# One rotary projection, exchanged rows and late division in the attention stage with heads of 64

## The chip, the core and the metric

The kernel runs on one core of one Trainium2 chip. The metric is the device time of one execution in microseconds, lower is better. A core has five engines that run side by side, each with its own queue of instructions, executed in order: TensorE (PE in the profile, its weight loads are PEld), VectorE (DVE), ScalarE (ACT), GpSimd (POOL) and SyncE (SP), which here issues nearly all DMAs. They wait for each other on semaphores. TensorE writes only to PSUM, which is divided here into tiles of 512 float32 columns ("banks") handed out in turn.

## The reference, cut to what matters

The program is four pairs of a feed-forward layer and an attention layer around 2048 tokens of 128 features. The change touches only the last attention layer, with 16 heads of 64, a latent of 64 for keys and values, rotary embedding and a causal mask:

```python
x = x + _L3_attn_ref(_layernorm(x), ...)

def _L3_attn_ref(x, wq, w_kv_down, w_k_up, w_v_up, wo):   # in outline
    lat = x @ w_kv_down.T                       # 2048 x 64
    q = rope(x @ wq.T)                          # 16 heads of 64
    k = rope(lat @ w_k_up.T)
    v = lat @ w_v_up.T
    p = softmax(causal(q @ k.T / 8))
    return (p @ v) @ wo.T

rope(t) = t * cos + rotate_half(t) * sin        # rotate_half exchanges the two halves of a head (32 rows), with a sign
```

## The kernel before, in words

The kernel is one list of stages (`STAGES`): feed-forward and attention by turns. Each stage is a generator that can begin ("lead") while the stage before still runs. The stage in question is `attn3`; `ffn3` runs before it (its first half-step) and after it.

`attn3` keeps features on the partitions and tokens along the free axis. Two heads make a pair of 2 x 64 = 128 rows, so there are `NP` = 8 pairs, and 2048 tokens are `NC` = 4 chunks of `CH` = 512. The 32 iterations `its` are (pair, chunk of queries).

*Making queries and keys.* `make(m)` yields the pieces of work that produce the rotated queries and keys of iteration m. Before the change there are four pieces (`half(what, i)`): each of q and k is projected twice, once with the weights and once with weights whose rows are exchanged by halves (`swapped` on the host). A projection of q takes three matmuls of 512 columns (`product`, lines 227 to 229: the operands are split into a high and a low part), one of k takes two (`latents`, lines 1753 and 1754). VectorE multiplies each projection, out of PSUM, with the cosine or the signed sine (line 1791), GpSimd adds the two products (`whole`, line 1801), and later ScalarE and GpSimd split the sum into high and low parts (`high`, lines 1806 and 1807), which go to DRAM and come back as rows of the score operands (`load`, line 1867). The pieces are emitted by `fill`, one per `SPACE` of a clock that counts matmul columns, up to `AHEAD` iterations in advance; deferred parts (`timed`) come `LATER` after. The pieces of the first three iterations are made in the lead, before the stage proper.

*The flash loops.* `flash` runs two streams on TensorE. Stream A computes the scores once (line 1069) to find the maxima of each query: VectorE reduces each pair of PSUM tiles (line 1087, `tc.high_priority()`), out of two double-width PSUM tiles (tag `s1`). Stream B computes the scores again, transposed (line 1171), ScalarE exponentiates (line 1179, tile `pt`, six buffers), and TensorE multiplies with the latent values (line 1136, `pv`). The sum of the exponentials is kept per partition in `sum`, one addition per exponential tile (`on_exp`, line 1993), half of them on GpSimd, half on VectorE, and the last ones of an iteration all on VectorE. Score tiles of stream B, projections (`rot`), totals (`sums`) and output products (`py`) share one ring of three PSUM banks (tag `s2`).

*Finishing an iteration.* `finish` copies `pv` to `ov`; `total` adds the sums over partitions by two matmuls with ones (line 2006). ScalarE copies the result, and its two distinct rows go to DRAM, come back spread over the partitions, VectorE takes 128 x 8 reciprocals (line 2026), which go to DRAM and come back broadcast; VectorE multiplies `ov` (line 2036), TensorE multiplies with the folded output weights `wo` (line 2042) and VectorE adds to the residual `xs` (line 2045). Only the last iteration takes the reciprocal in place (`direct`).

The order on every engine is set by the emission order, by priorities and by explicit ordering (`in_order`); buffers in rings decide what waits.

Of the kernel before, what the change touches and what calls it, by code (L numbers as in the profile page):

```python
# [64 lines left out]
def tile_macaron(ctx: ExitStack, tc: tile.TileContext, a: dict, out: bass.AP, stages=STAGES):  # L65
# [904 lines left out]
    def flash(io, pool, early, its, nh, causal, scale, s1, s2, pv_mm, put_max, begin, finish, poll=None,  # L970
# [60 lines left out]
        last_top = {}  # L1031
        alive = [True]
# [16 lines left out]
        def stream_a():  # L1049
            for n, (g, qc) in enumerate(its):  # L1050
# [4 lines left out]
                for pi in range(npair):  # L1055
                    for r in range(TC):
# [3 lines left out]
                        for kc in range(2 * pi, min(2 * pi + 2, nk)):  # L1060
                            for j0 in range(0, nh, 2):
# [14 lines left out]
                                with tc.high_priority():  # L1076
# [9 lines left out]
                                    else:  # L1086
                                        ins = nc.vector.tensor_reduce(  # L1087
                                            mp[:, r, j0 : j0 + 2, kc], both[:, :, :w], AX.X, ALU.max,
                                        )
                                if before is not None:  # L1090
                                    in_order(ins, before)
                                    before = None
# [11 lines left out]
        def stream_b():  # L1104
            pend = [None]

            def values(half=None):
# [4 lines left out]
                if halved:  # L1112

                    for j in range(2):
                        on_exp(n, kt, j, pts, c0)
# [591 lines left out]
    def pre_attn3(k, pool):  # L1707
        wdn = split(fetch(pool, "l3d", 0, P), pool, "wdn")
        return wdn, fetch(pool, "l3q", 0, 4 * P, "raw", 1)

    def attn3(io, k, w, early):
# [3 lines left out]
        SPACE, AHEAD, LATER, SHARE = 1300.0, 12, 9000.0, 2  # L1715
        RC, OUT = 5000.0, 8000.0
# [29 lines left out]
        def weights(p):  # L1746
            if p not in pw:
                raw = fetch(early, "l3q", p * 4 * P, (p + 1) * 4 * P, "raw", 1)
                pw[p] = split(raw, early, "pw", 1)
# [6 lines left out]
        def scratch(dt, name):  # L1756
            return early.tile([P, CH], dt, name=name, tag=name, bufs=2 if name == "rot0" else 1)
# [13 lines left out]
        def make(m):  # L1771
            p, c = its[m]
            halves = {}

            def half(what, i):
                while i == 0 and len(timed) > 1:
                    timed.pop(0)[1]()
                if what == "q" and i == 0:
                    halves["tabs"] = tabs_of.pop()
                    if c == 0:  # L1780
                        weights(p)
                wh, wl = pw[p]
                o = (2 * (what == "k") + i) * P
                w = tuple(t[:, o : o + P] for t in (wh, wl))
# [5 lines left out]
                t = scratch(F32R, f"rot{i}")  # L1790
                nc.vector.tensor_tensor(t.bitcast(F32), ps, halves["tabs"][i], ALU.mult)  # L1791
                halves[i] = t
                if i == 1:
                    if what == "k":
                        tabs_of.append(tables(scratch, "l3rope", (c + 1) % NC))
                    whole(what)

            def whole(what):
                t = halves[0]
                f = t.bitcast(F32)  # L1800
                nc.gpsimd.tensor_tensor(f, f, halves[1].bitcast(F32), ALU.add)
                timed.append((now[0] + LATER, lambda: high(what, t)))

            def high(what, t):
                h = early.tile([P, CH], F32R, name="h", tag="t", bufs=2)
                nc.scalar.copy(h, t.bitcast(F32))
                nc.gpsimd.tensor_tensor(t, t.bitcast(F32), h.bitcast(F32), ALU.subtract)
                nc.sync.dma_start(out=hl[what][m][: 2 * D, :], in_=h.bitcast(F32))
                nc.sync.dma_start(out=hl[what][m][2 * D :, :], in_=t.bitcast(F32))
# [3 lines left out]
            return [lambda what=what, i=i: half(what, i) for what in "qk" for i in range(2)]  # L1813
# [6 lines left out]
        for c in range(NC - 1):  # L1820
# [4 lines left out]
            for _ in range(4):  # L1825
                pieces.pop(0)()
                yield 4.0
                if timed:
                    timed.pop(0)[1]()
                    yield 1.0  # L1830
        yield True

        with tc.tile_pool(name="att0", bufs=1) as pool0, tc.tile_pool(name="att", bufs=1) as pool:
# [55 lines left out]
            def fill(clock, progress, always=False):  # L1889
# [5 lines left out]
                if pieces and (  # L1895
                    always or n_pieces - len(pieces) < n_pieces * progress + 4 * AHEAD
# [80 lines left out]
            inv = [dram.tile([2, CH], F32, name=f"inv{i}") for i in range(2)]  # L1977
            count = [0]

            def on_exp(n, kt, j, pts, c0):  # L1980
                if kt == 0:
                    sums[n, j] = pool.tile([P, CH], F32, name="sum", tag=f"sum{j}", bufs=2)
                    if its[n][1] == 0:
                        nc.vector.tensor_copy(sums[n, j], pts[j])
                    else:
                        first[n, j] = pts[j]
                    return
# [5 lines left out]
                eng.tensor_tensor(t[:, c0:], other[:, c0:], pts[j][:, c0:], ALU.add)  # L1993
# [3 lines left out]
            def finish(n, pv, after, pe):  # L1997
# [3 lines left out]
                rc = sums[n, 0]  # L2001

                def total():
                    ps = bank("sums")
                    for j in (1, 0):
                        pe(nc.tensor.matmul(  # L2006
                            ps[D * j : D * j + D, :], ones[:, :D], sums.pop((n, j)),
                            start=True, stop=True,
                        ))
                    nc.scalar.copy(rc, ps)  # L2010
                    if n == len(its) - 1:
                        after(0.0, lambda: direct(0))
                        return
                    nc.sync.dma_start(out=inv[n % 2], in_=rc[::D, :])
                    t = pool.tile([P, 2 * CH // P], F32, name="rc", tag="rc", bufs=2)
                    nc.sync.dma_start(out=t, in_=inv[n % 2].rearrange("j (p q) -> (j p) q", p=P // 2))
                    after(RC, lambda: inverse(t))

                def direct(i):
                    s = slice(i * P, (i + 1) * P)  # L2020
                    nc.vector.reciprocal(rc[:, s], rc[:, s])
                    nc.vector.tensor_tensor(ov[:, s], ov[:, s], rc[:, s], ALU.mult)
                    after(0.0, out_b if i + 1 == TC else lambda: direct(i + 1))

                def inverse(t):
                    nc.vector.reciprocal(t, t)
                    nc.sync.dma_start(out=inv[n % 2].rearrange("j (p q) -> (j p) q", p=P // 2), in_=t)
# [266 lines left out]
```

## Time and profile before

| | |
|---|---|
| time, median of 3 runs | 3750.55 us (3750.35 to 3751.68) |
| the profiled execution's own time | 3769.46 us |
| its span | 3767.7 us |
| PE busy over the span | 3420.8 us (91%) |
| DVE, ACT, POOL busy | 2870.9 us (76%), 2036.2 us (54%), 828.8 us (22%) |
| mean granted TensorE clock | 0.943 of full speed |

The profile is one execution, and its time lies 18.9 us above the median of the runs; sums are made within it. A row of a group reads: line, engine, operation, output<-inputs, shapes, count | busy us, mean ns of one | idle time of the engine just before, and what ended it. A row of the waits reads: who waited, for whom: us in total, times, longest us. A matmul on float32 shows as two records (two passes). Records overlap in the pipeline, so a cost on TensorE is read from start to start, not from the duration. Stage `attn3` proper lies between 2640 and 3627 us of the span.

### The profile page before, as it was taken

How to read it: one execution, taken by the hardware profiler on the slowest of the kernel's cores; microseconds unless marked ns; L12 is line 12 of the kernel's file. 1: busy time of each engine (PE TensorE's matmuls, PEld its weight loads, DVE VectorE, ACT ScalarE, POOL GpSimd, SP SyncE). 2: the span in 40 equal slices, each digit the busy share in tenths (PEclk: the TensorE clock that was granted, in tenths of full speed). 3: DMA queues.
4: the chain of work that ended last, by engine and by line, in shares of the span. 5: the costliest groups of instructions: out<-in, count | busy, mean ns of one | idle time of the engine just before them, and what ended most of it. 6: DMA issues, size and time to landing. Idle time of an engine off the chain costs nothing. (4 is left out here: it accounts for less than half of the span.)

```text
span 3767.7 us, 64628 instructions
## 1 busy us (share of the span) xinstructions
PE 3420.8 (91%) x25325; PEld 1846.5 (49%) x25325; DVE 2870.9 (76%) x4793; ACT 2036.2 (54%) x3838; POOL 828.8 (22%) x830
## 2 busy tenths in 40 slices
PE   7679987978999999996999999888999999999989
PEld 5543356863333333783333333366444444444458
DVE  6488555768999998668899999654777877788862
ACT  3246732325888888421788888732333444444442
POOL 1511124110000000112000000142555445533341
PEclk9779988987999999996999999998899999999999
DMA  3311023000000000102000000012443232221010
GB/s 104 83 49 29 9 81 95 4 26 5 12 12 14 8 3 1 35 1 70 10 14 6 16 5 4 15 46 75 140 147 112 97 106 97 89 63 52 24 34 12
DMA packets 124689, 170.18 MB, mean 45 GB/s; under 512 B 25120, under 2 KB 52514, under 8 KB 124384
## 3 DMA queue, kind: packets, MB, share of 16 engines
q1 hardware_dynamic: 121824, 160.80, 13.7%
q0 software_dynamic: 2560, 5.25, 0.9%
q8 instruction: 199, 3.26, 0.3%
q14 instruction: 106, 0.87, 0.1%
HBM read 101.25 MB, written 45.87 MB: 39 GB/s over the span
## 5 line engine op out<-in xcount | busy, mean ns | idle before, releaser
L1087 DVE TENSOR_REDUCE mp<-s 128x2 f32<-128x1024 f32 (+3 forms) x1440 | 1625.7, 1181 | 88.5 <-PE s L1069 68.1
L1199 ACT ACTIVATE pt<-s 128x512 f32<-128x512 f32 (+1 forms) x2368 | 1220.7, 601 | 216.4 <-PE s L1190 141.8
L1190 PE MATMUL s<-q,km 32*128 32x512 f32 (+2 forms) x2368 | 733.6, 491 | 28.6 <-ACT pt L1199 18.7
L1136 PE MATMUL pv<-pt,v 128*32 128x256 f32 (+1 forms) x8568 | 730.9, 413 | 22.9 <-ACT ov L1577 11.2
L1069 PE MATMUL s<-km,qt 32*128 32x512 f32 (+3 forms) x2368 | 620.0, 507 | 61.1 <-DVE mp L1087 37.1
L1190 PEld LDWEIGHTS s<-q,km 32*128 32x128 f32 (+1 forms) x2368 | 324.1, 184 | 531.6 <-issue 341.3
L1179 ACT ACTIVATE pt<-s 128x512 f32<-128x512 f32 (+3 forms) x640 | 306.2, 530 | 355.7 <-PE s L1171 212.8
L143 POOL TENSOR_TENSOR rs<-rs,minus_half 128x4 f32<-128x4 f32 x56 | 57.5, 1026 | 1543.7 <-DVE rs L142 1542.7
L1993 DVE TENSOR_TENSOR sum<-sum,pt 128x512 f32<-128x512 f32 (+3 forms) x328 | 259.4, 805 | 89.9 <-ACT pt L1179 88.3
L1136 PEld LDWEIGHTS pv<-pt,v 128*32 128x32 f32 x8568 | 169.1, 108 | 316.4 <-issue 146.3
L1171 PE MATMUL s<-q,k 64*128 64x512 f32 (+3 forms) x1920 | 300.0, 403 | 14.7 <-ACT pt L1179 10.4
L1136 PE MATMUL pv<-pt,latv 128*64 128x512 f32 (+3 forms) x1280 | 310.4, 564 | 1.3 <-ACT pt L1179 1.3
L1993 POOL TENSOR_TENSOR sum<-sum,pt 128x512 f32<-128x512 f32 (+1 forms) x200 | 265.6, 1328 | 181.5 <-ACT pt L1179 177.0
L1069 PEld LDWEIGHTS s<-km,qt 32*128 32x128 f32 (+1 forms) x2368 | 236.4, 191 | 124.1 <-DVE mp L1087 82.3
L1171 PEld LDWEIGHTS s<-q,k 64*128 64x128 f32 x1920 | 161.8, 188 | 224.8 <-issue 137.3
L715 ACT ACTIVATE sg<-pg 128x1024 f32<-128x1024 f32 x72 | 73.9, 1027 | 174.4 <-PE pg L229 158.8
L1069 PE MATMUL s<-k,q 64*128 64x512 f32 (+3 forms) x640 | 133.7, 433 | 19.0 <-DVE mp L1087 18.6
L1791 DVE TENSOR_TENSOR rot<-rot,tab 128x512 f32<-128x512 f32 x128 | 87.7, 685 | 74.2 <-PE rot L229 38.4
L725 PEld LDWEIGHTS pd<-l1d,h 128*128 128x128 f32 x1152 | 139.3, 192 | 5.6
L725 PE MATMUL pd<-l1d,h 128*128 128x128 f32 x1152 | 140.1, 275 | 0.0
L717 DVE TENSOR_TENSOR h<-pu,sg 128x1024 f32<-128x1024 f32 x72 | 87.9, 1220 | 60.6 <-PE pu L229 55.7
L1171 PE MATMUL s<-q,two 64*128 64x512 f32 (+3 forms) x640 | 128.0, 368 | 0.0
(575 smaller groups left out, 4696.7 us busy)
## 6 DMA issues: line engine op xcount, KB each, us to landing
tab<-in_l3rope SPq DMA_DIRECT2D x66, 256.0 KB
q<-q SPq DMA_DIRECT2D x32, 512.0 KB
k<-k SPq DMA_DIRECT2D x32, 512.0 KB
l0e<-in_l0e SPq DMA_DIRECT2D x32, 256.0 KB
q<-h SPq DMA_DIRECT2D x32, 256.0 KB
q<-rot SPq DMA_DIRECT2D x32, 256.0 KB
k<-h SPq DMA_DIRECT2D x32, 256.0 KB
k<-rot SPq DMA_DIRECT2D x32, 256.0 KB
```

Source lines behind the costliest of these rows:

```text
L715: nc.scalar.activation(sg, pg, AF.Silu)
L717: nc.vector.tensor_tensor(h.rearrange("p m n -> p (m n)"), pu, sg, ALU.mult)
L725: nc.tensor.matmul(pd[:, i, :], h[:, m, i * P : (i + 1) * P], wd[:, m, :], start=m == 0, stop=m == 1,)
L1069: pe(nc.tensor.matmul(ps[:, o : o + w], lhsT, rhs[:, :w], start=True, stop=not masked))
L1087: ins = nc.vector.tensor_reduce(mp[:, r, j0 : j0 + 2, kc], both[:, :, :w], AX.X, ALU.max,)
L1136: i = pe(nc.tensor.matmul(pv[out_rows, lo:hi], lhsT, pts[j][:, lo:hi], start=kt == 0, stop=kt == nt - 1 and hi == CH))
L1171: pe(nc.tensor.matmul(outs[j][:, c0:], lhsT, rhs[:, c0:], start=i == 0, stop=i == len(terms[0]) - 1 and not diag,))
L1179: ex = nc.scalar.activation(pts[j][:, c0:], outs[j][:, c0:], AF.Exp, scale=scale)
L1190: pe(nc.tensor.matmul(ps[:, c0:], lhsT, rhs[:, c0:], start=i == 0, stop=i == len(terms) - 1 and (tiled or not diag),))
L1199: ex = nc.scalar.activation(pt[:, c0:], ps[:, c0:], AF.Exp, scale=scale)
L1791: nc.vector.tensor_tensor(t.bitcast(F32), ps, halves["tabs"][i], ALU.mult)
L1993: eng.tensor_tensor(t[:, c0:], other[:, c0:], pts[j][:, c0:], ALU.add)
```

## The change

1. *One projection.* q and k are projected once per iteration (two pieces instead of four). ScalarE evicts the projection to SBUF; GpSimd multiplies it with the (rolled) sine into `u`; four DMAs exchange the row blocks of 32 from `u` to `v`; VectorE multiplies the projection with the cosine in place; GpSimd adds `v`, makes the high part and the low part. The weights fetched and split are half as many.
2. *Division behind the output product.* The sums are totalled by token: for each head and each 128 tokens one matmul with the sums as the stationary operand and one column of ones, which gives 128 x 8 values; VectorE inverts them directly. The output product is made for each head apart into two PSUM banks, ScalarE scales one by the inverse, VectorE scales and adds the other, GpSimd adds to the residual. The round trips through DRAM and the special last iteration go.
3. *Sums behind maxima.* Each sum on VectorE is ordered behind the latest maxima reduction emitted.
4. Pacing constants follow: `SPACE` 2600 instead of 1300, `LATER` 6000 instead of 9000, two pieces per iteration in the lead.

```diff
@@ flash
+                                        last_reduce.append(ins)
...
-                        on_exp(n, kt, j, pts, c0)
+                        ins = on_exp(n, kt, j, pts, c0)
+                        if ins is not None and last_reduce:
+                            in_order(ins, last_reduce[-1])
@@ attn3
-        SPACE, AHEAD, LATER, SHARE = 1300.0, 12, 9000.0, 2
-        RC, OUT = 5000.0, 8000.0
+        SPACE, AHEAD, LATER, SHARE = 2600.0, 12, 6000.0, 2
...
-            return early.tile([P, CH], dt, name=name, tag=name, bufs=2 if name == "rot0" else 1)
+            return early.tile([P, CH], dt, name=name, tag=name, bufs=1 if name in ("tab0", "tab1", "rot1") else 2)
...
-                t = scratch(F32R, f"rot{i}")
-                nc.vector.tensor_tensor(t.bitcast(F32), ps, halves["tabs"][i], ALU.mult)
...
+                t, u = scratch(F32R, "rot0"), scratch(F32, "rot1")
                 f = t.bitcast(F32)
-                nc.gpsimd.tensor_tensor(f, f, halves[1].bitcast(F32), ALU.add)
-                timed.append((now[0] + LATER, lambda: high(what, t)))
+                nc.scalar.copy(f, ps)
+                nc.gpsimd.tensor_tensor(u, f, kept["tabs"][1], ALU.mult)
+                nc.vector.tensor_tensor(f, f, kept["tabs"][0], ALU.mult)
+                v = scratch(F32, "rot2")
+                q = D // 2
+                for i in range(4):
+                    o = q * (i ^ 1)
+                    nc.sync.dma_start(out=v[q * i : q * i + q, :], in_=u[o : o + q, :])
...
+            def whole(what, t, v):
+                f = t.bitcast(F32)
+                nc.gpsimd.tensor_tensor(f, f, v, ALU.add)
                 h = early.tile([P, CH], F32R, name="h", tag="t", bufs=2)
-                nc.scalar.copy(h, t.bitcast(F32))
-                nc.gpsimd.tensor_tensor(t, t.bitcast(F32), h.bitcast(F32), ALU.subtract)
+                nc.gpsimd.tensor_scalar(h, f, 1.0, 0.0, ALU.mult, ALU.add)
+                nc.gpsimd.tensor_tensor(t, f, h.bitcast(F32), ALU.subtract)
@@ finish
-                    for j in (1, 0):
-                        pe(nc.tensor.matmul(
-                            ps[D * j : D * j + D, :], ones[:, :D], sums.pop((n, j)),
-                            start=True, stop=True,
-                        ))
-                    nc.scalar.copy(rc, ps)
...
+                        t = sums.pop((n, j))
+                        for i in range(TC):
+                            o = TC * j + i
+                            pe(nc.tensor.matmul(
+                                ps[:, o : o + 1], t[:, i * P : (i + 1) * P], ones[:, :1],
+                                start=True, stop=True,
+                            ))
+                    rc = pool.tile([P, 2 * TC], F32, name="rc", tag="rc", bufs=2)
+                    nc.vector.reciprocal(rc, ps[:, : 2 * TC])
+                    after(1500.0, lambda: out_b(rc))
+
+                def out_b(rc):
+                    outs = [bank("py").rearrange("p (i c) -> p i c", i=TC) for j in range(2)]
...
+                                outs[j][:, i, :], ov[rows, i * P : (i + 1) * P], wo[p][rows, :],
...
+                        nc.scalar.activation(y[:, i], outs[0][:, i], AF.Copy, scale=rc[:, i : i + 1])
+                    for i in range(TC):
+                        nc.vector.scalar_tensor_tensor(
+                            y[:, i], outs[1][:, i], rc[:, TC + i : TC + i + 1], y[:, i],
+                            op0=ALU.mult, op1=ALU.add,
                         )
...
-                    nc.vector.tensor_tensor(xs[qc], xs[qc], ps, ALU.add)
+                    nc.gpsimd.tensor_tensor(xs[qc], xs[qc], y, ALU.add)
```

## The prediction

> **What bounds the kernel now.** I read the page's first part, then the busy time by stretches of the changed stage (`attn3`: its burst of piece-making, the rest while pieces are made, and the end):
>
> ```profile
> core 0: us, PE busy (x) PEld busy (x) DVE busy (x) ACT busy (x) POOL busy (x), PEclk, DMA share, GB/s
> 2655.00:2797.00 142.00, 129.15 (x752) 62.98 (x751) 101.29 (x136) 51.58 (x102) 85.52 (x63) 0.95 0.41 137
> 2797.00:3300.00 503.00, 477.59 (x3184) 237.27 (x3186) 383.84 (x550) 208.93 (x422) 254.44 (x191) 0.98 0.32 105
> 3300.00:3627.00 327.00, 312.02 (x2300) 157.50 (x2296) 262.85 (x394) 145.32 (x299) 115.31 (x91) 0.99 0.12 38
> ```
>
> TensorE is busy 91 to 95%: it sets the pace, so a matmul less is time less. DVE comes second (71 to 80%); POOL stands at 60% in the burst. What still stops TensorE is in the waits of the stage (2640 to 3630 us):
>
> ```profile
> PEld s L1069 <- DVE mp L1087: 27.6, 43, 2.5
> PE s L1069 <- DVE mp L1087: 17.4, 22, 2.1
> PE pm L1967 <- DVE rot L1791: 5.8, 3, 2.9
> PEld rot L227 <- DVE rot L1791: 5.5, 6, 1.7
> ...
> ACT pt L1179 <- POOL sum L1993: 6.6, 3, 2.9
> ```
>
> TensorE waits for maxima (a late reduction holds a PSUM tile) and for rotary evictions on DVE. Waits of loads lie partly under running matmuls, so I count the first two rows as 25 us. For L1791 as releaser all TensorE rows add up to 26 us; I count 15. The last row: exponential tiles are held by GpSimd's sums only three times, so the six `pt` buffers have slack.
>
> The prices, from the timeline's PE rows (start to next start) and from groups:
>
> ```profile
> 2901.88 1.08 PE L2006 MATMUL sums<-sum,ones 128*64 128x512 f32 x4
> 2902.79 0.60 PE L1136 MATMUL pv<-pt,latv 128*64 128x512 f32 x2
> ```
> ```profile
> 639.09 0.97 PEld L678 LDWEIGHTS bank<-l1d,x2T 128*128 128x128 f32 x8 [0.18 <-DVE x2T L674]
> 639.98 0.19 PEld L229 LDWEIGHTS pu<-xTH,wgu8L 128*128 128x128 f32 x1
> ```
> ```profile
> L1801 POOL TENSOR_TENSOR rot<-rot,rot 128x512 f32<-128x512 f32 x58 | 80.5, 1387 | 144.1 <-DVE rot L1791 134.9 <-DVE mx L1095 6.8 <-ACT pt L1179 2.4
> L1807 POOL TENSOR_TENSOR rot<-rot,h 128x512 fp32r<-128x512 f32 x58 | 76.2, 1314 | 33.8 <-ACT h L1806 33.8
> ```
>
> **The change part by part.**
>
> *Projections removed.* A q projection runs from 2920.49 to 2921.38 (0.89 us, three matmuls), a k projection from 2932.74 to 2933.40 (0.66). One of each goes per iteration: 1.55 us, 0.78 per piece. Of 64 pieces 6 are made in the lead, 23 in or before the burst, 35 after.
>
> *Totals.* Before: 2901.88 to 2902.79, 0.91 to 0.96 us. After: 8 matmuls with a 128x128 float32 stationary operand, two passes each, so 16 weight loads for one column. The nearest row is L678, 8 columns behind such loads: 8 loads from 639.09 to 639.98, 0.112 us each. So 16 x 0.112 + 0.1 = 1.9 us: +0.94 per iteration, +30 us over 32. The Trainium skill (TensorEngine Tiling (Array Packing), Instruction Overhead) says that a matmul of one column costs as much as one of 60, about 60 cycles: at 2.4 GHz an estimate of 25 ns, 0.4 us for 16, a gain of 0.5 per iteration (-17 us). I take the trace: the load, not the column, sets the step. Ends: 1.7 us[...] and 3.0 (16 x 0.186, the duration of one load, if none overlaps).
>
> *Output product.* Before 8 records in 1.09 us. After 16, but the two heads lie in different halves of the rows; such pairs of L1171 start 4 ns apart, so 8 x 0.112 + 0.15: nothing gained. Two banks of the ring of three are now held. ScalarE frees the first after four scaled copies: 0.27 us (128x128 exponentials) to 0.48 (L161, scale and bias); with the 0.10 that L908's scale adds at 512 columns I take 0.37, so 1.5 us, 0.85 of it past the product. In the built order of TensorE 16 of 32 products stand directly ahead of a score pair that needs that bank: 16 x 0.85; another 10 follow a score pair or totals at once and wait about 0.8 for a bank. 22 us, less the 7 that waits on L2045 cost now; idle time here lets DVE catch up, so I take +12 (ends 0 and +25).
>
> *Evictions by ScalarE.* ACT is at 41 to 44%. A copy is 0.59 us (L2010's row), and the 15 us of waits on L1791 fall to about 4. After the burst: -7.
>
> *DVE.* Per iteration four L1791 (0.685), L2036 (0.876), L2045 (0.678) and L2026 (0.196) = 4.49 us go; two multiplications at 0.88 (L2036: two SBUF inputs), four scaled additions of 128x128 at 0.342 (L735) and a reciprocal of 0.195 come: 3.33. DVE was the cover of the maxima, not the bound, so this counts only through them. But the multiplication by the cosine is in place, so it waits until POOL has read the tile. In the built order it usually stands right behind a reduction whose matmul follows the projection on TensorE: DVE is there about 0.4 + 0.2 + 1.22 = 1.8 us after the projection, POOL is done after 0.2 + 0.3 + 0.59 + 1.3 + 0.3 (half a chance of a sum ahead) = 2.7. DVE stands 0.9 us with the next maxima and sums behind it, 35 times, 31 us; waits on the projection (36 us in the stage) and on `inv` (24) go. A quarter reaches TensorE: +8 (ends -5 and +25).
>
> *Sums behind maxima.* In the built order two thirds of DVE's sums move behind one to four reductions. Of the 25 us of waits on maxima I take back 8 (ends 0 and 15); a sum up to 1.2 us per reduction later is inside the slack of `pt`.
>
> *POOL.* Per piece before: L1801 and L1807, 2.70 us. After: product 1.39, addition 1.39, high part 0.69 (L872), low part 1.31: 4.78; and a residual addition of 1.28 per iteration. Over 800 us of the stage that is harmless (50% becomes 60%). In the burst it is not: between the 1st and 28th sum on POOL (142 us before) the built order has 21 of each rotary step (100 us), the same 27 sums (38), 3 residual additions (4), 2 weight splits (1): 144 us with the contention in these means, 134 at the shortest durations. Moreover `u` has one buffer: the next product waits until four DMAs (4 issues of 0.32, landing about 2.0: L2016 is issued until 2908.07, its reader starts at 2910.00) have read it: 3.3 us, of which one sum covers 1.4. Eight such places: 15 us. So 149 to 159; I take 153, +11, and TensorE's saving of 0.78 x 23 is lost there. If POOL kept pace the stretch would shrink by 14.
>
> *SP.* 256 exchange DMAs of 64 KB come, 155 issues of the `inv` trips go: 8 per iteration against 5. Key and query loads stand behind them, but are asked for up to 12 iterations ahead; without that cover each late load costs its 3 us. Lead: 6 x 0.78 = -5 of TensorE, +2 for POOL's waits ahead of `ffn3`'s high parts. End: four reciprocals of 0.92 go: -2.
>
> Sum: lead -3; burst +11; rest -27 (35 x 0.78) + 27 (29 totals) - 1 - 7 - 8 + 12 + 8 - 2 = +2. Together +10 on the profile's 3769.5: 3779.5, a factor 1.0027, which on the median 3750.55 is 3760.
>
> **The rivals.**
>
> *TensorE's saving arrives (faster).* POOL's lag fits into the `pt` slack and the ring hides the two output banks: lead -3, burst -14, rest -27 + 27 - 1 - 9 - 12 + 2 - 2 = -22: -39, 3712; with half of it 3730. For: PE is at 95% and every matmul counts. Against: POOL's 101% of the burst.
>
> *GpSimd becomes the bound beyond the burst (slower).* The three-step block of 3.4 us delays sums behind it; it decides once a sum is over 5 us late (two key tiles of slack). If half of the 58 pieces after the lead cost 1.5 us: +44 more, 3804. Against: three such waits now.
>
> *The load step overlaps for one column.* If the rule above holds, totals cost 47 us less: 3713. Against: row L678.
>
> *The parts cancel.* Within 0.2% (7.5 us), about what a measurement of this kernel can tell from no change. For: the sum of the rest is 2.
>
> **How the numbers follow.** Forecast (POOL-bound burst, rest even): 0.45, of which 0.36 above 3758 and 0.09 within; saving arrives 0.36 (0.33 faster, 0.03 within); POOL beyond the burst 0.14; cheap totals 0.05. Faster 0.38, same 0.12, slower 0.50. Likeliest 3760; its own range is 3745 to 3780. The range 3714 to 3806 leaves out a tenth at each side.
>
> **What would show it.** Right: POOL over 90% busy from about 2655 to 2810; totals near 1.9 us from start to start; DVE waiting for POOL at the cosine multiplication; maxima waits smaller after the last piece; score loads waiting on ACT's scaled copies. Wrong: totals near 0.5 us; the burst shorter than 142 us; POOL's sums releasing `pt` waits by tens of us late in the stage.

## The result and the profile after

The changed kernel took 3818.78 us, median of 4 runs (3816.82 to 3826.54), against 3751.11 (3750.35 to 3759.72, 4 runs) for the kernel before beside it: a ratio of 1.0179, 95% interval 1.0158 to 1.0199. It is slower by 67 us, which lies above the range of the prediction. The profiled execution took 3826.54 us, its span is 3824.8.

These are the three stretches of `attn3` in the changed kernel (the rows of before stand in the prediction). After the busy time of each engine come the granted clock of TensorE, the share of the DMA engines and what they moved.

```profile
core 0: us, PE busy (x) PEld busy (x) DVE busy (x) ACT busy (x) POOL busy (x), PEclk, DMA share, GB/s
2655.00:2797.00 142.00, 109.81 (x629) 57.22 (x628) 83.93 (x107) 43.50 (x91) 108.66 (x91) 0.82 0.47 150
2797.00:3300.00 503.00, 462.81 (x3301) 252.04 (x3301) 357.85 (x528) 207.14 (x451) 330.62 (x268) 0.93 0.35 110
3300.00:3627.00 327.00, 313.90 (x2367) 176.49 (x2363) 229.78 (x381) 142.45 (x312) 137.66 (x110) 0.96 0.13 43
```

In the burst (first row) TensorE fell from 129 to 110 us of 142, and its clock from 0.95 to 0.82. GpSimd rose from 85.5 to 108.7 us, which is 77% and not the "over 90%" that a bound by its rate would show. Every other engine became less busy. That points to waits in a ring of tiles and not to the rate of one engine.

These are waits of the changed kernel in the same stage, 2640 to 3690 us (who waited, for whom: us in total, times, longest). Some rows between them are left out:

```profile
DVE rot L1797 <- POOL rot L1796: 100.8, 45, 6.1
POOL x L2038 <- DVE y L2034: 74.2, 21, 10.9
POOL rot L1809 <- DMA rot<-rot: 64.9, 29, 4.6
PEld s L1175 <- ACT rot L1795: 43.3, 29, 6.8
PEld s L1175 <- ACT y L2032: 30.1, 37, 1.4
PE s L1175 <- ACT rot L1795: 22.5, 9, 6.5
PEld s L1070 <- DVE mp L1088: 17.4, 17, 2.1
PE s L1175 <- ACT y L2032: 15.6, 17, 1.0
PE s L1070 <- DVE mp L1088: 12.6, 14, 1.9
```

TensorE's waits for maxima fell from 27.6 + 17.4 to 17.4 + 12.6. In their place stand waits for ScalarE: for its copy of the projection (L1795) and for its scaled copies of the output product (L2032). VectorE stood 100.8 us for GpSimd's sine product (L1796), GpSimd 64.9 us for its own exchange and, in part 2's new residual addition (L2038), 74.2 us for VectorE.

What such a wait looks like is seen in the timeline of the burst (start, duration, engine, and in brackets the idle time before and who ended it; rows between are left out):

```profile
2770.41 0.59 ACT L1795 COPY rot<-rot 128x512 f32<-128x512 f32 x1 [2.11 <-DMA q<-rot]
2771.05 0.92 PEld L1175 LDWEIGHTS s<-q,k 64*128 64x128 f32 x5 [2.41 <-ACT rot L1795]
2771.05 0.62 POOL L1811 TENSOR_SCALAR h<-rot 128x512 fp32r<-128x512 f32 x1
2771.75 1.27 POOL L1812 TENSOR_TENSOR rot<-rot,h 128x512 fp32r<-128x512 f32 x1
2772.98 1.26 POOL L1796 TENSOR_TENSOR rot<-rot,tab 128x512 f32<-128x512 f32 x1
2774.26 2.41 SPq L1802 DMA_DIRECT2D rot<-rot  x4
2774.27 0.69 DVE L1797 TENSOR_TENSOR rot<-rot,tab 128x512 f32<-128x512 f32 x1 [5.40 <-POOL rot L1796]
2775.29 0.59 ACT L1795 COPY rot<-rot 128x512 f32<-128x512 f32 x1 [4.30 <-DMA k<-rot]
2775.93 2.28 PEld L2026 LDWEIGHTS py<-wvo,ov 64*128 64x128 f32 x16 [3.53 <-ACT rot L1795]
```

ScalarE's copy cannot start until one of the two `rot0` tiles is free, and that tile is freed by the last step of the piece two before it, whose work is a long chain: sine product, four DMAs, addition, high part, low part, store. While the copy stands at the head of ScalarE's queue, the exponentials stand behind it, the projection's PSUM bank is not freed, and the loads for the score and for the output product that need a bank wait 2.4 and 3.5 us on TensorE. VectorE, in its own queue, waits 5.4 us.

Two tables were worked out from the traces, and the experiments are read with them. The first is *progress*: the end of ScalarE's copy of `pv` for iteration n (`ov<-pv`) less the same in the kernel before, in us of the span. How far the lead has got at iteration 0 scatters from kernel to kernel, so differences along a row are read. There is one trace of each kernel; two traces of the same kernel (part 3, taken twice) give -12.5 and -22.4 us from iteration 0 to 31, so some 10 us along a whole row are not told from scatter.

| kernel | n=0 | 3 | 9 | 15 | 21 | 31 |
|---|---|---|---|---|---|---|
| changed kernel | -8.7 | 34.5 | 24.7 | 26.6 | 38.8 | 57.0 |
| part 1 (projection) | -18.5 | 24.3 | 22.3 | 32.7 | 37.7 | 34.4 |
| part 2 (division) | -12.1 | -8.7 | 4.0 | 17.8 | 31.5 | 57.2 |
| part 3 (order) | -12.4 | -14.4 | -18.3 | -22.1 | -16.6 | -24.9 |

The burst (n = 0 to 3) costs the changed kernel 43 us, all of it from part 1; from iteration 3 to 31 part 2 alone loses 66, about 2.3 per iteration. Part 1 shows no gain in that stretch, though its projections are shorter: +10, which is within the scatter.

The second is an *account of TensorE*: from iteration 0 to 31, the time from each matmul record's start to the next one's, summed by product. Idle time falls to the product ahead of it.

| product, us | before | changed | part 1 | part 2 | part 3 |
|---|---|---|---|---|---|
| projections `rot` | 92.8 | 47.5 | 51.6 | 97.2 | 93.8 |
| totals `sums` | 30.7 | 59.0 | 30.3 | 60.3 | 29.5 |
| output product `py` | 33.0 | 44.0 | 35.6 | 44.9 | 34.0 |
| scores B of queries and keys | 242.6 | 286.5 | 275.0 | 268.1 | 241.2 |
| `pv` | 292.4 | 307.5 | 315.9 | 295.3 | 296.9 |
| all else | 265.6 | 278.3 | 301.6 | 260.6 | 249.2 |
| sum | 957.1 | 1022.8 | 1010.0 | 1026.4 | 944.6 |

The saving arrived in full: 45 us of projections are gone. The totals gave back 28 and the output product 11, so the change's own work on TensorE comes to -6. Against these -6 stand 72 us that go to the same matmuls as before: they take longer, with idle time and a lower clock inside them, and the sum is +66.

### The profile page after: what moved, and what is told of

Same layout as the page of the kernel before. It is cut to its first block, busy times and chain, and to the rows that moved or that the text cites. A ratio compares the mean times of both kernels' runs of the same rounds, so it can differ in the third digit from the quotient of the medians.

```text
span 3824.8 us, 65985 instructions
## 1 busy us (share of the span) xinstructions
PE 3453.6 (90%) x25805; PEld 1906.7 (50%) x25805; DVE 2832.8 (74%) x4787; ACT 2053.7 (54%) x3934; POOL 988.7 (26%) x990
## 3 DMA queue, kind: packets, MB, share of 16 engines
q1 hardware_dynamic: 120100, 168.03, 14.4%
## 4 chain that ended last, share of the span: by engine, by line
PE 60%; DVE 9%; POOL 7%; ACT 4%; DMA 4%; issue 3%; SPq 2%; POOLq 0%; DVEq 0%; ACTq 0%
PE pv L1140 19%; PE s L1194 12%; PE s L1175 6%; DVE mp L1088 4%; PE pd L725 3%; ACT pt L1203 2%; PE s L1070 2%; PE bank L227 2%; PE bank L228 2%; PE bank L229 2%; DMA rot<-rot 2%; POOL sum L1996 1%; PE sums L2013 1%; SPq L1802 1%; POOL rot L1796 1%
## 5 line engine op out<-in xcount | busy, mean ns | idle before, releaser
L1194 PE MATMUL s<-q,km 32*128 32x512 f32 (+2 forms) x2368 | 735.7, 494 | 28.6 <-ACT pt L1203 18.6
L1175 PE MATMUL s<-q,k 64*128 64x512 f32 (+3 forms) x1920 | 320.4, 419 | 42.0 <-ACT rot L1795 22.5
L1140 PE MATMUL pv<-pt,latv 128*64 128x512 f32 (+3 forms) x1280 | 321.0, 583 | 11.3 <-ACT pt L1183 11.2
L1175 PEld LDWEIGHTS s<-q,k 64*128 64x128 f32 x1920 | 172.1, 196 | 248.4 <-issue 106.4
L1996 DVE TENSOR_TENSOR sum<-sum,pt 128x512 f32<-128x512 f32 (+3 forms) x328 | 245.4, 769 | 18.5 <-ACT pt L1183 11.3
L1070 PE MATMUL s<-k,q 64*128 64x512 f32 (+3 forms) x640 | 143.1, 438 | 14.9 <-DVE mp L1088 14.7
L1797 DVE TENSOR_TENSOR rot<-rot,tab 128x512 f32<-128x512 f32 x64 | 69.1, 1080 | 104.5 <-POOL rot L1796 104.4
L1175 PE MATMUL s<-q,two 64*128 64x512 f32 (+3 forms) x640 | 137.1, 382 | 0.0
```

What stands on the lines that cost most here:

```text
L1070: pe(nc.tensor.matmul(ps[:, o : o + w], lhsT, rhs[:, :w], start=True, stop=not masked))
L1140: i = pe(nc.tensor.matmul(pv[out_rows, lo:hi], lhsT, pts[j][:, lo:hi], start=kt == 0, stop=kt == nt - 1 and hi == CH))
L1175: pe(nc.tensor.matmul(outs[j][:, c0:], lhsT, rhs[:, c0:], start=i == 0, stop=i == len(terms[0]) - 1 and not diag,))
L1194: pe(nc.tensor.matmul(ps[:, c0:], lhsT, rhs[:, c0:], start=i == 0, stop=i == len(terms) - 1 and (tiled or not diag),))
L1996: ins = eng.tensor_tensor(t[:, c0:], other[:, c0:], pts[j][:, c0:], ALU.add)
```

## The experiments

Three theories stood first. *S*: ScalarE's copy waits for the store of the low part, because eviction tile and low part are one tile. *B*: the two output banks and the totals carry the loss. *P*: GpSimd's work per piece sets the burst. The kernels are the kernel before with one part of the change, or the changed kernel with one edit. Ratios are to the kernel before on the same chip.

**Each part alone.** Part 1 keeps the old division and order, part 2 the old projection and order, part 3 only adds `in_order(ins, last_reduce[-1])` behind VectorE's sums.

> Part 1 alone (one projection, rows exchanged by DMA, its pacing; division and order of the sums as before). Theory S (ScalarE's eviction waits until a store has read the old low part out of the same ring of two tiles, and the exponentials stand behind it): 1.55 us of TensorE per iteration go (50 us), the stall of about 48 us read in the burst of the changed kernel comes, so about even: 3740 to 3760, with all loss before 2850 us and a gain of 0.7 to 1.5 us per iteration after it. Theory B (the two output banks and the totals carry most of the loss): the projection alone is faster, 3700 to 3725.

> Part 2 alone (division behind the output product). Theory B: per iteration +0.92 for totals (1.88 against 0.96 from start to start in the changed kernel), -0.17 for the output product, and 1.5 us at each product that stands directly ahead of a score pair (half of them), so about 1.5 to 2.1 us times 32: +48 to +67, 3800 to 3818. Theory S: this part is small, +10 to +25, and most of the 68 us belong to the projection.

> Part 3 alone (sums on VectorE behind the latest maxima reduction). Both theories: waits of TensorE on maxima fall, -5 to -12 us (3739 to 3746). If the sums come so late that exponential tiles are held, 0 to +10 instead, and waits of ACT on DVE's sums appear.

Measured: part 1 3806.17 us, ratio 1.013 (1.0103 to 1.0158); part 2 3824.63, 1.0177 (1.0154 to 1.0199); part 3 3742.95, 0.996 (0.9948 to 0.9972). Two of the three parts lose and the smallest gains. Part 1 missed both ranges: the loss of the burst came as theory S had it, the gain behind it did not. Part 2 lies at the upper end of theory B's range. Alone they add to +49, +66 and -15 us against the changed kernel's +67, so they overlap: in part 1 alone TensorE waited 57.1 + 40.7 us for maxima, in the whole change 17.4 + 12.6.

**The low part in another tile** (theory S): GpSimd writes the low part into `v`, and it is stored from there, so the tile of ScalarE's copy is free before the store.

```diff
-                nc.gpsimd.tensor_tensor(t, f, h.bitcast(F32), ALU.subtract)
+                nc.gpsimd.tensor_tensor(v, f, h.bitcast(F32), ALU.subtract)
...
-                nc.sync.dma_start(out=hl[what][m][2 * D :, :], in_=f)
+                nc.sync.dma_start(out=hl[what][m][2 * D :, :], in_=v.bitcast(F32))
```

> The changed kernel, but GpSimd writes the low part into the tile of the exchanged rows and it is stored from there, so the eviction tile is free as soon as GpSimd has read it; nothing else changes. Theory S: the 70 us for which ACT waits on the stores go, 32 to 48 us come back: 3770 to 3787. Theory P (GpSimd is over 100% of the burst and sets it whatever the ring does): 3808 to 3818, the burst stays at about 34 us over before.

Measured: 3838.57 us, ratio 1.0211 (1.0185 to 1.0236), no faster. The copy waited as before, only for another step of the same chain (waits of this kernel, 2640 to 3690 us):

```profile
ACT rot L1795 <- POOL rot L1812: 81.9, 20, 8.1
```

Theory S falls as it stood: the store was merely last, and the tile is held by the whole chain of the piece two before. The edit is not quite clean, since `v` is now held until the store and the next exchange into it must wait. A third tile in the ring of `rot0`, the direct test of this account, was not run.

**Parts 1 and 3**, to see what the order cures.

> Parts 1 and 3 together, with the old division through DRAM. The projection alone cost +50 us and the order alone gained 13. If the two are independent: +37, near 3790 us. If the order also takes away the waits for maxima that the projection brought (its VectorE standing for GpSimd with reductions queued behind it): 3765 to 3780, and the time lost after the burst disappears while the burst's loss (about +24 us by the fourth iteration) stays.

Measured: 3807.81 us, ratio 1.0098 (1.0081 to 1.0115): additive (1.3% less 0.4). The waits for maxima stayed at 41.5 + 28.2 us, so the second half of the expectation was wrong. They are 17.4 + 12.6 only when part 2 is added. Why is not shown: part 2 takes the division's trips through DRAM out of VectorE's queue (37.0 + 26.0 us of waits here), but at half the rate, below, these waits are high with part 2 in as well.

**Cosine straight out of PSUM.** VectorE reads the bank itself; ScalarE's copy is for GpSimd alone. The sine tile `u` (`rot1`) gets two buffers instead of one, and `v` (`rot2`) one instead of two.

```diff
-            return early.tile([P, CH], dt, name=name, tag=name, bufs=1 if name in ("tab0", "tab1", "rot1") else 2)
+            return early.tile([P, CH], dt, name=name, tag=name, bufs=2 if name in ("rot0", "rot1") else 1)
...
-                nc.scalar.copy(f, ps)
-                nc.gpsimd.tensor_tensor(u, f, kept["tabs"][1], ALU.mult)
-                nc.vector.tensor_tensor(f, f, kept["tabs"][0], ALU.mult)
+                nc.scalar.copy(u, ps)
+                nc.vector.tensor_tensor(f, ps, kept["tabs"][0], ALU.mult)
+                nc.gpsimd.tensor_tensor(u, u, kept["tabs"][1], ALU.mult)
```

> As the kernel with parts 1 and 3, but VectorE multiplies by the cosine straight out of PSUM into a tile of its own, and ScalarE's copy is GpSimd's alone (sine product in place). VectorE no longer waits for GpSimd, and the tile that ScalarE fills is held until four DMAs have read it instead of until the low part is made. Theory G (GpSimd's chain reaches TensorE through two waits, VectorE's at the cosine and ScalarE's at its copy): faster than the kernel with parts 1 and 3 by 20 us or more, about 3750, with no wait of VectorE on GpSimd's sine product and ScalarE's copies waiting under 20 us in all. Rival R (GpSimd's rate alone, more than 100% busy in the burst, sets the loss, whoever stands for it): within 8 us of the kernel with parts 1 and 3.

Measured: 3788.68 us, ratio 1.0058 (1.0036 to 1.0079), from 1.0098: 0.4%, 15 us less. That lies between both theories, and the interval of the difference (about 10 us to either side) reaches both; the changed rings are part of it. ScalarE's wait for DMAs is nearly gone (8.0 us, from 35.6 + 29.8), but in the burst TensorE now waits for VectorE at the same ring of tiles (42.1 + 34.5 us on L1797 in the stage): progress still loses 30 us from iteration 0 to 3. The product itself became cheaper too. This is VectorE's group in the changed kernel and then in this one:

```profile
L1797 DVE TENSOR_TENSOR rot<-rot,tab 128x512 f32<-128x512 f32 x57 | 61.1, 1072 | 101.0 <-POOL rot L1796 100.8
```
```profile
L1797 DVE TENSOR_TENSOR rot<-rot,tab 128x512 f32<-128x512 f32 x57 | 38.8, 681 | 40.3 <-DMA k<-rot 22.4 <-DMA q<-rot 11.8 <-ACT rot L1796 3.0
```

**Half the rate of pieces** in the changed kernel: `SPACE` 5200 instead of 2600.

> The changed kernel with pieces emitted at half the rate (SPACE 5200 instead of 2600), so that the burst is twice as long and GpSimd is asked for about half as much in it. If GpSimd's rate in the burst makes the loss of some 44 us (progress at the fourth iteration against the kernel before): 25 to 35 us of it go, 3785 to 3795. If the eviction's own latency (copy, product, DMAs, each piece) makes it, the loss is per piece and stays: 3810 to 3822.

Measured: 3824.25 us, ratio 1.0156 (1.0125 to 1.0187). The loss of the burst vanished (progress -8.2 at iteration 0, -11.9 at 3) and came back by iteration 15 (+26.6, where the changed kernel also stands). Pacing moves the cost; each piece still brings it. In the whole stage VectorE now stood 122.3 us for GpSimd, and TensorE 52.0 + 41.6 us for maxima, which VectorE computes (2640 to 3690 us):

```profile
DVE rot L1797 <- POOL rot L1796: 122.3, 44, 6.2
PEld s L1070 <- DVE mp L1088: 52.0, 33, 5.7
PE s L1070 <- DVE mp L1088: 41.6, 30, 5.3
```

**The exchange left out** of the changed kernel: GpSimd adds the sine product unexchanged, with two buffers for it.

```diff
-                t, u = scratch(F32R, "rot0"), scratch(F32, "rot1")
+                t, u = scratch(F32R, "rot0"), scratch(F32, "rot2")
...
-                v = scratch(F32, "rot2")
-                q = D // 2
-                for i in range(4):
-                    o = q * (i ^ 1)
-                    nc.sync.dma_start(out=v[q * i : q * i + q, :], in_=u[o : o + q, :])
+                v = u
```

> The changed kernel without the four exchange DMAs: GpSimd adds the sine product itself, unexchanged (that part of the computation is left out). GpSimd's work per piece stays 4.8 us, TensorE's, ScalarE's and VectorE's too. If GpSimd's rate makes the burst's loss: +30 us or more at the fourth iteration remain, ratio 1.015 to 1.018. If the exchange's way through the queue of SyncE and back (GpSimd standing for it 65 us, with ScalarE's two tiles held) makes it: the loss at the fourth iteration falls under +10, ratio 1.006 to 1.011.

Measured: 3804.39 us, ratio 1.014 (1.0114 to 1.0166). The time lies between both ranges; the burst answers clearly: progress went from -10.0 at iteration 0 to +2.5 at 3, so 12.5 us were lost instead of 43. GpSimd was now busy for most of the burst:

```profile
2655.00:2797.00 142.00, 121.25 (x716) 62.37 (x712) 87.27 (x117) 50.44 (x104) 124.42 (x104) 0.86 0.39 136
```

It is busy 124.4 us of 142 where the changed kernel had 108.7, while doing 104 operations instead of 91. So of the burst's 43 us some 31 came of the exchange, its way through SyncE's queue and back with the tiles held meanwhile, and of the single buffer of `u`, which this edit doubles as well; the two are not separated. Some 12 stay, with GpSimd busy 88%. VectorE's standing for GpSimd was not the price: up to 2850 us it is 55.9 us here, 50.1 in the changed kernel. The whole time moved by about 15 us only (1.0179 to 1.014), less than the burst.

**The totals spread** (part 2 alone): the second head's matmuls are emitted 1500 columns after the first's.

> Part 2 alone with the totals of the two heads at two moments, 1500 columns of other matmuls apart, instead of one behind the other; the work of TensorE is the same. Theory K (eight matmuls of one column, 1.9 us, leave the array nearly idle and trip its clock: 14 of the 16 intervals of lower clock after the burst follow totals): the lowered clock goes, and with it half of some 70 us of cold time less the 30 of the kernel before, so about 20 us: 3800 to 3808. Theory B (two output banks of a ring of three held by ScalarE and VectorE): nothing gained, one more bank request per iteration, 3824 to 3835.

Measured: 3839.5 us, ratio 1.0175 (1.0149 to 1.0202), the same as part 2. The last stretch, in part 2 and with the totals spread:

```profile
3300.00:3627.00 327.00, 311.79 (x2316) 171.60 (x2314) 237.25 (x378) 137.61 (x305) 124.38 (x98) 0.95 0.11 36
```
```profile
3300.00:3627.00 327.00, 311.59 (x2439) 171.38 (x2440) 243.28 (x394) 145.31 (x319) 131.15 (x103) 1.00 0.14 45
```

Theory K was right about the clock here, and wrong about the gain. From iteration 0 to 31 the time at half clock fell from 92 to 55 us, worth 19 us, but the account is only 6 us shorter (1026.4 to 1020.6). In it the output product fell from 44.9 to 35.5 us, but the totals rose from 60.3 to 65.5 and the scores from 268.1 to 276.6, with the waits on ScalarE's scaled copies up from 26.8 + 14.3 to 34.9 + 23.7: this fits the one more bank that is asked for per iteration. Outside the stage this execution spent 27 us more at half clock than that of part 2, so the equal times, which are known to about 13 us, do not say that a lower clock is free.

**Half the totals** (part 2 alone): those of the second head are left out, and its output product is divided by the first head's.

> Part 2 alone, with the totals of the second head left out (its output product is divided by those of the first): 4 matmuls of one column per iteration instead of 8, everything else as it was. If the totals' 1.9 us of TensorE are on the path: -0.94 x 32 = -30 us, and if half the length no longer trips the clock, some 20 more: ratio to the kernel before 1.004 to 1.010 instead of 1.018. If the two output banks carry the loss: 1.014 to 1.018.

Measured: 3801.31 us, ratio 1.0071 (1.005 to 1.0092), from 1.0177: 40 us less, and in the account the totals fell from 60.3 to 32.9, the sum from 1026.4 to 983.9. Four matmuls of one column less per iteration bring 27 us by their own time and some 10 more in the scores and `pv` (268.1 + 295.3 to 262.2 + 291.1). Of the edits tried, this is the strongest lever in part 2.

**Output banks freed by one instruction**, and the same with the totals spread. GpSimd does the rest of the scaling in SBUF.

```diff
-                    for i in range(TC):
-                        nc.scalar.activation(y[:, i], outs[0][:, i], AF.Copy, scale=rc[:, i : i + 1])
...
+                    nc.scalar.copy(y, outs[0])
+                    nc.vector.tensor_tensor(
+                        z, outs[1], rc[:, TC : 2 * TC].unsqueeze(2).to_broadcast([P, TC, C]), ALU.mult,
+                    )
+                    nc.gpsimd.tensor_tensor(
+                        y, y, rc[:, :TC].unsqueeze(2).to_broadcast([P, TC, C]), ALU.mult,
+                    )
+                    nc.gpsimd.tensor_tensor(y, y, z, ALU.add)
```

> Part 2 alone, but each output bank is freed by one instruction of 512 columns: ScalarE copies the first (0.59 us instead of four scaled copies of 0.37), VectorE multiplies the second by the broadcast inverse (0.7 instead of four of 0.34), and GpSimd multiplies and adds the rest in SBUF. TensorE's work is the same. Theory B (the held banks are on the path): the 25 to 43 us of score loads and products waiting on the scaled copies fall under 10, and the time by 17 to 25 us: ratio 1.011 to 1.013. Theory K (the clock after the totals is what counts): 1.016 to 1.018, since the totals stay in one piece.

> Both: the totals of the two heads 1500 columns apart, and each output bank freed by one instruction. Splitting alone took the cold time after 2860 us from 85 to 27 us and moved the time by nothing, with the wait on the scaled copies grown from 17 to 28 us. If the two costs are additive and stand for each other: only the totals' own +30 us is left, ratio 1.007 to 1.010. If neither is on the path: 1.016 to 1.018.

Measured: 3841.29 us, ratio 1.0188 (1.015 to 1.0226), and 3841.62, 1.0176 (1.0139 to 1.0212). The wait on the held banks fell by half and nothing was gained. Part 2, then with the banks freed early (2640 to 3690 us):

```profile
PEld s L1171 <- ACT y L2026: 26.8, 32, 1.7
PE s L1171 <- ACT y L2026: 14.3, 18, 1.4
```
```profile
PEld s L1171 <- ACT y L2026: 15.7, 25, 1.2
PE s L1171 <- ACT y L2026: 5.7, 12, 0.8
```

Theory B finds no support as far as the banks go: this wait seems to have stood in place of another one (in the account `pv` rose from 295.3 to 300.1 where the scores fell from 268.1 to 262.3). A wait named last is not yet a cost. The interval would still hide a gain of about 12 us, and GpSimd's added work (its queue stood 79.1 us for ScalarE's copy in the first of the two, 27.1 in the second) may have taken some back.

**Parts 1 and 3 with cosine out of PSUM at half the rate**; then with the exchange emitted 2000 columns later; then with the exchange left out (the sine product is added unexchanged). All three keep the buffers of the kernel with cosine out of PSUM.

> Parts 1 and 3 with VectorE's cosine product straight out of PSUM, at half the rate of pieces (SPACE 5200). Halving the rate took the burst's loss away (progress at the fourth iteration -12 instead of +34 us against the kernel before) but the same time was lost in the next ten iterations, with VectorE standing for GpSimd 122 us and 49 us more of waits on maxima. Theory W (after the burst the loss is that standing, and nothing else): with it gone the time lands at or under that of part 3 alone, ratio 0.988 to 0.996. Theory L (each piece costs TensorE about 1.6 us by its eviction's latency, wherever it is placed): the loss only moves, ratio 1.003 to 1.007.

> The last kernel of parts 1 and 3 (cosine out of PSUM, half the rate), with the exchange DMAs emitted 2000 columns later. In that kernel VectorE stood 77 us for the division's two trips through DRAM between 2800 and 3250 us (15 in the kernel before), maxima queued behind; SyncE's queue stood 127 us for GpSimd's sine product ahead of an exchange. Theory Q (the exchange, waiting for GpSimd, holds the division's trips behind it in SyncE's queue): VectorE's waits on the trips fall under 40 us, those of TensorE on maxima from 57 to about 30, ratio 0.994 to 0.999. Theory D (the trips are late because the DMA engines are busier, whatever the order of issue): ratio 1.001 to 1.005.

> The mended kernel of parts 1 and 3 (cosine out of PSUM, half the rate) without the four exchange DMAs (GpSimd adds the sine product unexchanged; that part of the computation is left out). It bounds what one projection could bring if the exchange were free: TensorE's 45 us of projections are gone and nothing takes their place. If the exchange (its place in SyncE's queue, the division's trips behind it, GpSimd standing for it) is the whole price: ratio 0.980 to 0.988, VectorE's waits on the division's trips back under 25 us. If GpSimd's 4.8 us per piece cost by themselves: 0.994 or more.

Measured: 3782.94 us, ratio 1.0031 (1.0019 to 1.0043); 3761.47, 1.0021 (1.0009 to 1.0032); 3716.02, 0.9908 (0.9894 to 0.9922).

| kernel, progress | n=0 | 3 | 9 | 15 | 21 | 31 |
|---|---|---|---|---|---|---|
| out of PSUM, half rate | -3.1 | -16.4 | -9.3 | 20.0 | 26.8 | 17.4 |
| exchange later | -16.5 | -28.9 | -21.2 | 3.2 | 1.6 | -7.9 |
| no exchange | -16.1 | -39.1 | -47.0 | -40.8 | -48.5 | -57.1 |

The first fits theory L: the loss moved behind the burst (+36 between iterations 3 and 15). The two rows of the division's trips in VectorE's waits (2800 to 3250 us) are what theory Q is about. They stood at 39.4 and 37.5 us; with the exchange emitted later:

```profile
DVE ov L2046 <- DMA sum<-inv: 34.4, 11, 5.6
DVE rc L2036 <- DMA rc<-inv: 23.1, 9, 5.8
```

That is 57.5 instead of 76.9, and the ratio moved by 0.1%, inside the intervals and in theory D's range: Q is at best a small part. And with no exchange at all VectorE still waited 33.2 + 12.9 us for the trips, while the kernel was faster than any other; most of their lateness was a companion, not the cause. What went is the exchange's part in each piece, 1.2% of the time, 46 us. It didn't become the 0.980 to 0.988 expected, so the exchange is not the whole price; that GpSimd's longer work per piece is the remainder was not tested.

**All parts, cosine out of PSUM, half the rate.**

> All three parts, with VectorE's cosine product straight out of PSUM and half the rate of pieces. The account of TensorE's time by product gives -45 us of projections, +28 of totals and +11 of output products from the first to the last iteration, together -6; the rest of the changed kernel's +66 is idle time and a lowered clock. If the burst's chain and VectorE's standing for GpSimd are all of that rest: ratio 1.000 to 1.006. If the output banks and the totals' own waits are on the path besides (they were worth 27 us in part 2 alone): 1.008 to 1.013.

Measured: 3781.15 us, ratio 1.0076 (1.0051 to 1.0101), on the edge between the two. From iteration 3 to 9 it runs level with the kernel before (-28.6 to -26.7); from 9 to 31 it loses 38. More than half of the change's loss (1.0 of 1.8%) was the way the eviction was built and paced. Of the 0.76% that stay, the same kernel without part 2 has 0.31.

**Part 3 once more.**

> Part 3 alone once more, beside the mended kernel without the exchange and in more rounds, as the version that beats both kernels: 0.994 to 0.998 as before.

Measured: 3740.14 us, ratio 0.9967 (0.9955 to 0.9978). It is the fastest kernel with the whole computation, ahead of both.

## Why the prediction was wrong

The sign was right, the size was not: +10 on the profile was forecast, and the profiles differ by 57 us (3826.54 against 3769.46), the medians by 68. In the table of progress the lead came to -9 us (forecast: -3), the burst to +43 (forecast: +11) and the rest to +22 (forecast: +2).

*Burst, +11: the failed step.* The prediction took GpSimd's rate and its waits for `u` as the bound (149 to 159 us for what took 142), with GpSimd over 90% busy. It was busy 77%, and 43 us were lost. Missing was the ring: ScalarE's copy is queued ahead of exponentials and waits for a tile which GpSimd's chain of the piece two before still holds. I had named one buffer of that chain, `u`, with 15 us for GpSimd, but asked only what GpSimd waits for, not who stands for GpSimd. The exchange and the one buffer of `u` made some 31 of the 43 us. The 12.5 us lost without them look like the +11, but that is chance: without the waits for `u` the prediction's own terms give 144 us for 142.

*ScalarE's evictions, -7.* The waits on VectorE's evictions were to fall from 15 us to 4; in their place stand 43.3 + 22.5 us of waits on ScalarE. But 28.6 + 22.5 of them lie before 2850 us and belong to the burst. Behind it, where this term was meant, loads waited 14.8 us, none over 0.8, and no matmul did: it stays unconfirmed and is not refuted. What was wrong is the ground given for it, for ScalarE's 42% of busy time says nothing about a wait at the head of its queue.

*VectorE standing for GpSimd, +8.* I estimated 0.9 us for 35 pieces, 31 us; behind 2850 us it stood 50.8 us, up to 6.1 at a time, and as long again before. Taking that wait away, with a cheaper product and other rings, was worth 15 us in parts 1 and 3, with some 10 to either side.

*Rotary, -27 after the burst and the saving in it.* Right: 45.3 us by the account against 0.78 x 58 pieces = 45.

*Totals, +27.* Right to a us: 16 records run from 3494.78 to the next product at 3496.65, 1.87 us, and the account has +28.3.

```profile
3494.78 1.95 PE L2013 MATMUL sums<-ones,sum 128*128 128x1 f32 x16
3496.65 1.63 PE L1175 MATMUL s<-q,k 64*128 64x512 f32 x6
```

The row of loads behind 8 columns held, and the estimate of 0.4 us by 60 cycles for one column did not. In effect the term may have been too small: with half the totals gone 40 us went where 30 were expected, known to about 11.

*Output product, nothing.* The product took 11 us more in the account, 7 to 8 of them clock: 15.4 us of it ran at half clock, none before.

*Two output banks, +12.* The wait came where the built order had put it: a product, a score on the third bank, and the second score 1.5 us later.

```profile
3500.58 1.16 PE L2026 MATMUL py<-wvo,ov 64*128 64x128 f32 x16
3501.49 0.47 PE L1175 MATMUL s<-q,k 64*128 64x512 f32 x1
3502.97 0.96 PE L1175 MATMUL s<-q,k 64*128 64x512 f32 x5 [1.00 <-ACT y L2032]
```

45.7 us of such waits stand in the trace, but halving their like in part 2 brought nothing that could be measured, so this term is not confirmed as a cost.

*Sums behind maxima, -8.* Right, a little small: -12 to -15 us alone.

*The clock, not counted.* By the three stretches' rows TensorE lost (1 - 0.82) x 142 + (1 - 0.93) x 503 + (1 - 0.96) x 327 = 74 us to a lower clock, before 7 + 10 + 3 = 20. The Trainium skill (TensorE: Matmul & The Clock Gate, Part 1) says that the clock falls to half when a window of about 3.4 us was idle. The single waits here, 2.4 to 3.5 us in the timeline above and 6.8 us at the longest, are of that order; that such a wait alone lowers the clock is not shown. The clock is a follower as much as a cause: with spread totals 19 us of it came back in the stage and only 6 us of time. How much of the 54 us would be won by the clock alone stays open.

Of the rivals, "GpSimd becomes the bound beyond the burst" (3804) came nearest in size, though not by its mechanism: the sums on GpSimd released `pt` only six times, 8.0 us in all. What the sum missed in the burst was not a price of an instruction but queues behind a waiting one. Why the rest lost 22 us and not 2 is known only in part: part 2 alone loses 66 there, and in part 2 leaving out half the totals brought 40 us, freeing the banks nothing measurable.

## What to carry to other kernels

When an eviction (the copy that empties a PSUM bank) is moved to another engine, ask when its destination tile comes free, and count the whole chain that holds it (here product, DMAs, addition, two splits) against the ring's depth times the distance between pieces; an engine at 42% still stops everything behind the instruction that waits. An operation in place on two engines is a wait for the slower one. Undo each part by itself: the smallest edit of this change, the order of the sums, was the only one that paid, and a wait that is named last in a trace is a cost only when removing it moves the time.

## What the runs showed of the hardware

- VectorE's product took 0.68 us with an operand in PSUM and 1.07 on average with both in SBUF: 0.69 while GpSimd stood idle, 1.75 beside its addition (the starts 2774.27 and 2779.65 in the changed kernel). Of its 64 products 33 ran with GpSimd idle for nine tenths of the time or more, and none of them took over 0.69; the other 31 took 1.50 on average. The Trainium skill (GPSIMD Engine Reference, Specifications) lists this contention for instructions with two SBUF inputs; the prediction had priced the product at 0.88.
- A group of 16 loads for one column each, though TensorE is never idle in it, goes with a lower clock: of 16 intervals of half clock (71.7 us) between 2860 and 3640 us in part 2 alone, 14 began within 7 us behind such a group, and with the groups spread 3 intervals (27.3 us) were left. With half the totals there were 5 (27.3 us).
- A lowered clock was not all time to be had: with the groups spread, time at half clock from iteration 0 to 31 fell from 92 to 55 us, worth 19 us, and the account of TensorE fell by 6.
